# Softmax sums by a chain of adds, one ones product per batch, and a normalization that takes two head groups at a time

## The chip, the cores and the metric

The kernel runs on one core of one Trainium2 chip. TensorE (PE in the profile) does the matrix products, VectorE (DVE), ScalarE (ACT) and GpSimd (POOL) the elementwise work, and SyncE (SP) issues most transfers. The metric is the device time of one execution in microseconds; lower is better. The time before is given as the median of three runs.

## What is computed

Two sequences of 1024 rows of 1024 numbers pass through half a feed-forward layer (a base product plus a gated low-rank part), a causal attention with 32 query heads and 8 key/value heads, and the same half feed-forward layer again. Each of the three parts adds to the residual stream and starts with a layer norm. The change lies in the attention alone:

```python
qg = q.reshape(B, N_KV_HEADS, GROUP, T, D_HEAD)
att = jnp.einsum('bhgqd,bhkd->bhgqk', qg.astype(jnp.float32), k.astype(jnp.float32)) / math.sqrt(D_HEAD)
causal = jnp.tril(jnp.ones((T, T), dtype=bool))
att = jnp.where(causal[None, None, None], att, -jnp.inf)
probs = jax.nn.softmax(att, axis=-1).astype(resid.dtype)
ctx = jnp.einsum('bhgqk,bhkd->bhgqd', probs, v)
```

`GROUP` is 4, `D_HEAD` 32, T 1024.

## The kernel before

The 2048 rows are 16 tiles of 128 rows (t = 0 to 15), eight per sequence. The attention goes through them in the order 0 to 7, 9 to 15, 8; one such stretch of time is called the step of tile t here. A tile sees L = t mod 8 + 1 key tiles, so L runs from 1 to 8. Inside a step, the eight key/value heads are called groups, g = 0 to 7; a group holds four query heads. A (tile, group, key tile) triple is a unit; there are 576 of them.

For each unit, TensorE makes the scores twice: a first time (`unit_s1`, L645) for the row maxima, which VectorE reduces out of PSUM (L662), and a second time (`unit_s2`, L796) with the maxima folded into the operands, from which ScalarE takes the exponentials `p32` (L802), a tile of 128 keys by four heads of 128 queries in float32. On the diagonal key tile GpSimd clears what the causal mask forbids (L804). Between the units, pieces of dense work for neighbouring tiles are dealt out (`step`): feed-forward products, the q/k/v products, the output projection (L404 to L406), three half-precision products for each block of 128.

The weights `p32` are gathered by `av_add` into batches of up to `BATCH = 4` key tiles of one group: batches of 4 and 4 for L = 8, of 4 and 3 for L = 7, of 4 and 1 for L = 5, one batch for L up to 4. When a later batch has begun, `add_pairs` adds the batch's weights two by two on VectorE (L718, tile `pair`, two buffers); an odd one is left as it is. When the later batches hold `SKEW = 2` units, `av_batch` issues the batch's products on TensorE (L739): for each key tile four products with the value tile, one for each head in its own 32 columns of the array, into `av[:, 0, :]`, and then for each pair (or odd left-over) four products with a block of ones, into `av[:, 1, :]`, which so collects the softmax denominators, equal in all 32 rows of a head. A float32 product shows as two instructions in the profile, so one such set of four heads is eight of them. The products of a batch are tied in order (`issue_after`) and have high priority.

After the last batch of a group comes its normalization (L745 to L757): ScalarE copies both halves of `av` to SBUF (L746), VectorE takes the reciprocal of the 128x128 sums (L748) and multiplies (L753), ScalarE rounds the result to half precision (L754, `c.high(g)`), and GpSimd subtracts to get the low part (L755, `c.low(g)`). The two halves of eight groups are the operand of the output projection (`stage_c1`). The PSUM pool `p_av` has one buffer, which takes a whole bank whatever the tile's size; the next group's first product has to wait until the copy L746 has read it. The pool is also used by the first feed-forward passes (`ffn` with `first`).

The framework builds the order of instructions on each engine at compile time: it simulates a timeline with its own costs and takes, for each engine, what is ready in that timeline, by priority. Within an engine the chip then runs that fixed order and waits wherever an operand is late. Where two engines touch one PSUM tile, the framework puts a wait between them.

Of the kernel before, what the change touches and what calls it, by code (L numbers as in the profile page):

```python
# [9 lines left out]
FP = mybir.dt.float32  # L10
# [3 lines left out]
ALU = mybir.AluOpType  # L14
# [3 lines left out]
NH, NKV, DH, GRP = 32, 8, 32, 4  # L18
E, R = 8, 16
P = 128  # L20
KB = D // P
# [20 lines left out]
def kernel(  # L42
# [16 lines left out]
    nc = tc.nc  # L59
# [5 lines left out]
    small = ctx.enter_context(tc.tile_pool(name="small", bufs=SB))  # L65
# [11 lines left out]
    p_av = ctx.enter_context(tc.tile_pool(name="p_av", bufs=1, space=bass.MemoryType.PSUM))  # L77
# [321 lines left out]
    def dense(ps, tt, wsel, n=512, last=True):  # L399

        for k in range(KB):
            wh, wl = wsel(k)
            th, tl = tt.high(k), tt.low(k)
            nc.tensor.matmul(ps, lhsT=th, rhs=wh, start=(k == 0), stop=False)  # L404
            nc.tensor.matmul(ps, lhsT=th, rhs=wl, start=False, stop=False)  # L405
            nc.tensor.matmul(ps, lhsT=tl, rhs=wh, start=False, stop=(last and k == KB - 1))  # L406
            if k % 2 == 1:
                yield
# [26 lines left out]

    def ffn(xt, tt, done, first=False):
        if first:
            psa = p_av.tile([P, 2, P], FP, name="av").rearrange("p a q -> p (a q)")
        else:
            psa = p_dense.tile([P, 512], FP, name="pd")  # L440
        yield from dense(psa[:, 0 : P + E], tt, lambda k: (ag[:, 0, k, :], ag[:, 1, k, :]))
        nc.gpsimd.dma_start(out=xt, in_=hb.partition_broadcast(P), accum_op=ALU.add)

        lg = small.tile([P, E], FP, name="lg")
        nc.scalar.activation(lg, psa[:, P : P + E], AF.Copy, scale=S["cg"])
        nv = small.tile([P, 1], FP, name="nv")
        nc.vector.tensor_reduce(nv, lg, AX.X, ALU.max, negate=True)
        ex = small.tile([P, E], FP, name="ex")
        nc.scalar.activation(ex, lg, AF.Exp, bias=nv)
        fe = lg.unsqueeze(1).to_broadcast([P, E, E])  # L450
        ee = lg.unsqueeze(2).to_broadcast([P, E, E])
        lw = small.tile([P, E, R], FP, name="lw", bufs=1)
        gt, eq = lw[:, :, 0:E], lw[:, :, E : 2 * E]
        nc.vector.tensor_tensor(gt, fe, ee, ALU.is_gt)
        nc.vector.tensor_tensor(eq, fe, ee, ALU.is_equal)
        nc.vector.tensor_tensor(eq, eq, tri, ALU.mult)
        nc.vector.tensor_tensor(gt, gt, eq, ALU.add)
        rk = small.tile([P, E], FP, name="rk")
        nc.vector.tensor_reduce(rk, gt, AX.X, ALU.add)
        nc.vector.scalar_tensor_tensor(ex, rk, 1.5, ex, ALU.is_lt, ALU.mult)  # L460
        sm = small.tile([P, 1], FP, name="sm")
        nc.vector.tensor_reduce(sm, ex, AX.X, ALU.add)
        nc.vector.reciprocal(sm, sm)
        nc.vector.tensor_scalar(ex, ex, sm, S["inva2"], ALU.mult, ALU.mult)
        nc.vector.tensor_tensor(
            lw, psa[:, 0:P].rearrange("p (e r) -> p e r", r=R),
            ex.unsqueeze(2).to_broadcast([P, E, R]), ALU.mult,
        )
        yield True
        psb = [None, None]  # L470
        lh = ll = None
        for n in range(2):
            ps = p_dense.tile([P, 512], FP, name="pd")
            psb[n] = ps
            yield from dense(
                ps, tt, lambda k: (wb[:, n, 0, k, :], wb[:, n, 1, k, :]), last=False
            )
            if n == 0:
                pst = p_s1.tile([P, GRP, P], FP, name="s1")[:, 0, :]
                nc.tensor.transpose(pst, lw.rearrange("p e r -> p (e r)"), ident)  # L480
                lh = small.tile([P, P], HP, name="lh", bufs=LB)
                ll = small.tile([P, P], HP, name="ll", bufs=LB)
                nc.scalar.copy(lh, pst)
                nc.vector.tensor_tensor(ll, pst, lh, ALU.subtract)
                yield
            c = bass.ts(n, 512)
            nc.tensor.matmul(ps, lhsT=lh, rhs=lbh[:, c], start=False, stop=False)  # L487
            nc.tensor.matmul(ps, lhsT=lh, rhs=lbl[:, c], start=False, stop=False)
            nc.tensor.matmul(ps, lhsT=ll, rhs=lbh[:, c], start=False, stop=True)
            yield  # L490
            nc.vector.scalar_tensor_tensor(xt[:, c], ps, S["uf", n], xt[:, c], ALU.mult, ALU.add)  # L491
            done(n)
            if n == 0:
                yield True

    def stage_a1(t):
        tt = layernorm(xts[t], turn=t < NTURN)
        yield

        def done(n):  # L500
            if n == 1:
                Ts["x2", t] = layernorm(xts[t])
                if t == LATE:
                    late["x"] = dram.tile([P, D], FP, name="xlate")
                    nc.sync.dma_start(out=late["x"], in_=xts.pop(t))

        yield from ffn(xts[t], tt, done, first=t < NTURN)
        yield True
# [24 lines left out]
    KT, VA, QS, CTX, CT = {}, {}, {}, {}, {}  # L533
# [168 lines left out]
    avt = [None]  # L702

    pairs = {}

    def add_pairs(batch):

        t, g, L, us = batch
        key = (t, g, us[0][0])
        if key in pairs:  # L710
            return
        pairs[key] = []
        for i in range(0, len(us), 2):
            if i + 1 == len(us):
                pairs[key].append(us[i][1])
                continue
            sums = pp.tile([P, GRP, P], FP, name="pair", bufs=2)
            nc.vector.tensor_tensor(sums, us[i][1], us[i + 1][1], ALU.add)  # L718
            pairs[key].append(sums)

    def av_batch():

        add_pairs(pend[0])
        t, g, L, us = pend.popleft()
        if us[0][0] == 0:
            avt[0] = p_av.tile([P, 2, P], FP, name="av")
        av = avt[0]
        last = us[-1][0] == L - 1
        runs = [(0, VA[t - t % TPB + j][:, g, :], p32) for j, p32 in reversed(us)]
        runs += [(1, ones, sums) for sums in reversed(pairs.pop((t, g, us[0][0])))]  # L730
        prev = None
        for n, (i, w, p32) in enumerate(runs):
            for h in range(GRP):
                rows = slice(h * DH, (h + 1) * DH)
                with ExitStack() as st:
                    if prev is not None:
                        st.enter_context(tc.high_priority())
                        st.enter_context(tc.issue_after(prev.ins))
                    prev = nc.tensor.matmul(  # L739
                        av[rows, i, :], lhsT=w, rhs=p32[:, h, :],  # L740
                        start=(us[0][0] == 0 and n == 0), stop=(last and n == len(runs) - 1),
                        skip_group_check=True, tile_position=(0, h * DH),
                    )
        if last:
            o = pp.tile([P, 2, P], FP, name="o", bufs=2)  # L745
            nc.scalar.copy(o, av)  # L746
            rc = o[:, 1, :]
            nc.vector.reciprocal(rc, rc)  # L748
            if t not in CTX:
                CTX[t] = Halves()  # L750
            c = CTX[t]
            o2 = pp.tile([P, P], FP, name="o2", bufs=1)
            nc.vector.tensor_tensor(o2, o[:, 0, :], rc, ALU.mult)  # L753
            nc.scalar.copy(c.high(g), o2)  # L754
            nc.gpsimd.tensor_tensor(c.low(g), o2, c.high(g), ALU.subtract)  # L755
            if g == NKV - 1:
                CT[t] = CTX.pop(t)  # L757

    def av_add(t, g, j, L, p32):

# [65 lines left out]
    def stage_c2(t):  # L826
        xt = xts[t]

        def done(n):
            if t == LATE:  # L830
                c = bass.ts(n, 512)
                nc.sync.dma_start(out=of[bass.ts(t, P), c], in_=xt[:, c])
            elif n == 1:
                nc.sync.dma_start(out=of[bass.ts(t, P), :], in_=xt)

        yield from ffn(xt, Ts.pop(("x3", t)), done)
        xts.pop(t)
        for u in {LATE - 1: (t + 5, t + 6), NT - 5: (LATE,), LATE: ()}.get(t, (t + 5,)):
            if u < NT:
                load_x(u)  # L840
        yield True
# [89 lines left out]
    pp = ctx.enter_context(tc.tile_pool(name="pp", bufs=2, reuse_waits="tile"))  # L931
# [5 lines left out]
    def flush(_):  # L937
        while pend:
            av_batch()
        yield True  # L940
# [198 lines left out]
```

## Time and profile before

| what | value |
|---|---|
| median of three runs (lowest, highest) | 1507.35 us (1506.07, 1509.0) |
| profiled execution, first to last instruction | 1508.5 us |
| mean granted TensorE clock | 0.978 of full speed |
| second-score products L796 | 576 of 128x512, 385 ns each |
| exponentials L802 | 576 of 128x512, 688 ns each |
| maxima L662, PSUM source | 480 of 128x512, 675 ns each |
| normalization on ScalarE and GpSimd: L746, L754, L755 | 128 each; 372, 297 and 521 ns |

The profiled execution is one execution under the hardware profiler; its span lies 1.2 us above the median of the three runs. Each group of instructions is given by its line, and `out<-in` names the tiles. The duration of a TensorE product contains its way through the array; products follow one another faster than that (in the timeline, dense products of 128x512 start 0.22 us apart and are listed with 0.38 us each), so costs on TensorE are better taken from starts than from durations. The idle time behind the bar in a group's line is what the engine stood still before those instructions, with what ended it.

### The profile page before, as it was taken

Reading aid. Unit: us, or ns where it says so; the run is one execution under the profiler, and the core shown is the slowest. Engines: PE = TensorE matmul, PEld = TensorE weight load, DVE = VectorE, ACT = ScalarE, POOL = GpSimd, SP = SyncE. Lnnn points to the kernel's source line nnn. Section 1 sums busy time; section 2 is a strip of 40 time slices with the busy share of each in tenths; the row PEclk is TensorE's granted clock in tenths of the full one; section 3 lists DMA queues with packets and bytes.
Section 4 is the critical chain, followed back from the end, with each engine's and each line's share of the span. In section 5 each row is a group of like instructions: output and inputs, shape, how many; then the busy total and the mean of one; then the engine's idle time right before and its main releaser. Section 6 shows DMA issues by size and latency. Waiting matters only on the chain.

```text
span 1508.5 us, 35338 instructions
## 1 busy us (share of the span) xinstructions
PE 1407.3 (93%) x14596; PEld 787.6 (52%) x14596; DVE 1136.9 (75%) x2411; ACT 749.4 (50%) x1356; POOL 388.6 (26%) x642
## 2 busy tenths in 40 slices
PE   5877889989999999999999898999999999989998
PEld 3333445545555555565654454555555556556544
DVE  6876957777869789688863687886869689789753
ACT  8563435444545455465561334553645456556531
POOL 3442224222322222222120133322322122221120
PEclk9998999999999999999999899999999999999999
DMA  8989187468487874846658858669595863923552
GB/s 294 324 193 245 24 214 192 141 166 261 90 285 87 237 186 85 258 114 141 192 145 269 181 185 239 188 162 264 105 297 78 242 162 87 275 82 86 127 163 76
DMA packets 265266, 269.40 MB, mean 179 GB/s; under 512 B 227472, under 2 KB 230544, under 8 KB 245392
## 3 DMA queue, kind: packets, MB, share of 16 engines
q1 hardware_dynamic: 259024, 239.87, 57.3%
q0 software_dynamic: 4640, 16.78, 6.5%
q10 hardware_dynamic: 1440, 10.49, 1.9%
q8 instruction: 114, 1.87, 0.5%
q14 instruction: 48, 0.39, 0.1%
HBM read 191.60 MB, written 20.45 MB: 141 GB/s over the span
## 4 chain that ended last, share of the span: by engine, by line
PE 68%; DVE 13%; DMA 10%; ACT 3%; issue 3%; POOL 1%; SPq 1%; ACTq 0%; DVEq 0%; POOLq 0%
PE pd L404 13%; PE pd L405 13%; PE pd L406 13%; PE av L739 11%; PE s L796 6%; PE s L645 6%; DMA ws<-wstr 4%; DVE mx L662 4%; DMA tt<-hl 3%; DVE pair L718 2%; DMA qt<-qst 1%; DVE o L748 1%; ACT p L802 1%; DVE bst L374 1%; PE pd L487 1%
## 5 line engine op out<-in xcount | busy, mean ns | idle before, releaser
L802 ACT ACTIVATE p<-s,cs 128x512 f32<-128x512 f32 x576 | 380.8, 688 | 266.9 <-PE s L796 260.4
L662 DVE TENSOR_REDUCE mx<-s 128x4 f32<-128x512 f32 x480 | 315.5, 675 | 55.7 <-PE s L645 45.4
L718 DVE TENSOR_TENSOR pair<-p,p 128x512 f32<-128x512 f32 x256 | 178.0, 697 | 62.3 <-ACT p L802 30.9
L645 PE MATMUL s<-kts,qt 96*128 96x128 f16 x2304 | 217.9, 221 | 7.1 <-DVE mx L662 2.6
L796 PE MATMUL s<-qt,kts 128*128 128x512 f16 x576 | 211.0, 385 | 11.8 <-ACT p L802 5.8
L404 PE MATMUL pd<-ws,tt 128*128 128x512 f16 x544 | 208.8, 384 | 14.1 <-DMA ws<-wstr 11.5
L645 PEld LDWEIGHTS <-qt 96*128 96x128 f16 x2304 | 165.4, 99 | 100.7 <-issue 30.1
L405 PE MATMUL pd<-ws,tt 128*128 128x512 f16 x544 | 208.2, 383 | 0.0
L406 PE MATMUL pd<-ws,tt 128*128 128x512 f16 x544 | 207.3, 382 | 0.0
L404 PE MATMUL pd<-wb,tt 128*128 128x512 f16 x512 | 197.9, 387 | 8.5 <-DVE xt L491 5.0
L404 PEld LDWEIGHTS <-tt 128*128 128x128 f16 x1312 | 130.5, 99 | 139.3 <-DMA tt<-hl 14.9
L405 PE MATMUL pd<-wb,tt 128*128 128x512 f16 x512 | 197.1, 385 | 1.4 <-DVE wb L213 1.4
L405 PEld LDWEIGHTS <-tt 128*128 128x128 f16 x1312 | 130.8, 100 | 128.7 <-issue 24.2
L406 PE MATMUL pd<-wb,tt 128*128 128x512 f16 x512 | 197.1, 385 | 0.0
L406 PEld LDWEIGHTS <-tt 128*128 128x128 f16 x1312 | 130.5, 100 | 125.0 <-issue 10.6
L739 PE MATMUL av<-p,va 128*32 128x128 f32 x4608 | 166.9, 278 | 4.6 <-ACT o L746 2.6
L804 POOL TENSOR_SCALAR_AFFINE_SELECT p<-p 128x512 f32<-128x512 f32 x128 | 90.7, 712 | 234.9 <-ACT p L802 228.3
L739 PEld LDWEIGHTS av<-p,va 128*32 128x32 f32 x4608 | 115.6, 110 | 68.1 <-issue 52.9
L755 POOL TENSOR_TENSOR tt<-o,tt 128x128 f16<-128x128 f32 x128 | 66.6, 521 | 325.9 <-ACT tt L754 325.8
L748 DVE RECIPROCAL o<-o 128x128 f32<-128x128 f32 x128 | 120.8, 944 | 21.4 <-ACT o L746 21.2
L657 POOL TENSOR_SCALAR_AFFINE_SELECT sm<-sm 128x512 f32<-128x512 f32 x96 | 66.2, 689 | 203.1 <-ACT sm L656 198.0
L754 ACT CAST tt<-o 128x128 f16<-128x128 f32 x128 | 38.0, 297 | 110.0 <-DVE o L753 105.8
(203 smaller groups left out, 1891.1 us busy)
## 6 DMA issues: line engine op xcount, KB each, us to landing
ws<-wstr SPq DMA_DIRECT2D x142, 1024.0 KB, 5.8
xt<-hb POOLq DMA_DIRECT2D x32, 512.0 KB, 6.3
wstr<-ws ACTq DMA_DIRECT2D x9, 1024.0 KB, 6.1
xt<-in_x_dram SPq DMA_DIRECT2D x16, 512.0 KB, 3.9
out_dram<-xt SPq DMA_DIRECT2D x15, 512.0 KB, 2.9
ws<-in_wb_dram SPq DMA_DIRECT2D x2, 1024.0 KB, 8.7
qst<-in_wb_dram SPq DMA_DIRECT2D x2, 1024.0 KB, 13.2
st<-in_wo_dram SPq DMA_DIRECT2D x2, 1024.0 KB, 14.4
```

Source lines behind the costliest of these rows:

```text
L404: nc.tensor.matmul(ps, lhsT=th, rhs=wh, start=(k == 0), stop=False)
L405: nc.tensor.matmul(ps, lhsT=th, rhs=wl, start=False, stop=False)
L406: nc.tensor.matmul(ps, lhsT=tl, rhs=wh, start=False, stop=(last and k == KB - 1))
L645: nc.tensor.matmul(ps[:, h, :], lhsT=q[0 : 3 * DH, h, :], rhs=KT[b0 + j][0 : 3 * DH, g, :], start=(not pem or h == 0), stop=not pem,)
L662: nc.vector.tensor_reduce(mx[:, odd, j, :], ps, AX.X, ALU.max)
L718: nc.vector.tensor_tensor(sums, us[i][1], us[i + 1][1], ALU.add)
L739: prev = nc.tensor.matmul(av[rows, i, :], lhsT=w, rhs=p32[:, h, :], start=(us[0][0] == 0 and n == 0), stop=(last and n == len(runs) - 1), ...
L748: nc.vector.reciprocal(rc, rc)
L755: nc.gpsimd.tensor_tensor(c.low(g), o2, c.high(g), ALU.subtract)
L796: ins = nc.tensor.matmul(ps.rearrange("p h k -> p (h k)"), lhsT=KT[b0 + j][:, g, :], rhs=q.rearrange("p h k -> p (h k)"), start=True, stop ...
L802: nc.scalar.activation(p32, ps, AF.Exp, scale=cs)
L804: nc.gpsimd.affine_select(out=p32, in_=p32, compare_op=ALU.is_ge, fill=0.0, base=0, pattern=[[0, GRP], [1, P]], channel_multiplier=-1,)
```

## The change

`add_pairs` adds all weights of a batch, up to four, one after another into one tile `pair`, which now has three buffers; a batch of one is left as it is. So `av_batch` has one ones product (eight instructions) for each batch. The PSUM tile `av` holds two neighbouring groups, even and odd, 128x512 in all, and the normalization runs once for the two, after the odd one's last batch. It copies the two value halves on ScalarE, transposes the two sum halves in blocks of 32x32 on VectorE straight from PSUM, takes the reciprocal of one column for each block (eight numbers in a row of the tile), spreads each back over 32 columns in a second transpose, multiplies, rounds and subtracts. Its working tile is one buffer of `pair`; the tiles `o` and `o2` are gone.

```diff
@@ ffn
-            psa = p_av.tile([P, 2, P], FP, name="av").rearrange("p a q -> p (a q)")
+            psa = p_av.tile([P, 2, 2, P], FP, name="av").rearrange("p g a q -> p (g a q)")
@@ add_pairs
-        pairs[key] = []
-        for i in range(0, len(us), 2):
-            if i + 1 == len(us):
-                pairs[key].append(us[i][1])
-                continue
-            sums = pp.tile([P, GRP, P], FP, name="pair", bufs=2)
-            nc.vector.tensor_tensor(sums, us[i][1], us[i + 1][1], ALU.add)
-            pairs[key].append(sums)
+        if len(us) == 1:
+            pairs[key] = [us[0][1]]
+            return
+        sums = pp.tile([P, GRP, P], FP, name="pair", bufs=3)
+        nc.vector.tensor_tensor(sums, us[0][1], us[1][1], ALU.add)
+        for _, p32 in us[2:]:
+            nc.vector.tensor_tensor(sums, sums, p32, ALU.add)
+        pairs[key] = [sums]
@@ av_batch
-        if us[0][0] == 0:
-            avt[0] = p_av.tile([P, 2, P], FP, name="av")
-        av = avt[0]
+        odd = g % 2
+        if us[0][0] == 0 and not odd:
+            avt[0] = p_av.tile([P, 2, 2, P], FP, name="av")
+        av = avt[0][:, odd]
...
-        if last:
-            o = pp.tile([P, 2, P], FP, name="o", bufs=2)
-            nc.scalar.copy(o, av)
-            rc = o[:, 1, :]
-            nc.vector.reciprocal(rc, rc)
-            if t not in CTX:
-                CTX[t] = Halves()
-            c = CTX[t]
-            o2 = pp.tile([P, P], FP, name="o2", bufs=1)
-            nc.vector.tensor_tensor(o2, o[:, 0, :], rc, ALU.mult)
-            nc.scalar.copy(c.high(g), o2)
-            nc.gpsimd.tensor_tensor(c.low(g), o2, c.high(g), ALU.subtract)
-            if g == NKV - 1:
-                CT[t] = CTX.pop(t)
+        if last and odd:
+            normalize(t, g - 1, avt[0])
+
+    def normalize(t, g, av):
+
+        w = pp.tile([P, GRP, P], FP, name="pair", bufs=3)
+        o, rc = w[:, 0:2, :], w[:, 2:4, :]
+        nc.scalar.copy(o, av[:, :, 0, :])
+        nc.vector.transpose(rc, av[:, :, 1, :])
+        r = small.tile([P, 2 * P // DH], FP, name="rcol")
+        nc.vector.reciprocal(r, rc.rearrange("p a (b q) -> p (a b) q", q=DH)[:, :, 0])
+        nc.vector.transpose(rc, r.unsqueeze(2).to_broadcast([P, 2 * P // DH, DH]))
+        if t not in CTX:
+            CTX[t] = Halves()
+        c = CTX[t]
+        nc.vector.tensor_tensor(o, o, rc, ALU.mult)
+        hi, lo = c.tt[:, g : g + 2, :], c.tt[:, KB + g : KB + g + 2, :]
+        nc.scalar.copy(hi, o)
+        nc.gpsimd.tensor_tensor(lo, o, hi, ALU.subtract)
+        if g == NKV - 2:
+            CT[t] = CTX.pop(t)
```

## The prediction

> **What bounds the kernel now.** I read the page's busy shares and the chain of waits first, then the engines' busy time step by step, then the groups that the change touches, and last the waits.
>
> ```profile
> PE 1407.3 (93%) x14596; PEld 787.6 (52%) x14596; DVE 1136.9 (75%) x2411; ACT 749.4 (50%) x1356; POOL 388.6 (26%) x642
> PE 68%; DVE 13%; DMA 10%; ACT 3%; issue 3%; POOL 1%; SPq 1%; ACTq 0%; DVEq 0%; POOLq 0%
> PE pd L404 13%; PE pd L405 13%; PE pd L406 13%; PE av L739 11%; PE s L796 6%; PE s L645 6%; DMA ws<-wstr 4%; DVE mx L662 4%; DMA tt<-hl 3%; DVE pair L718 2%; DMA qt<-qst 1%; DVE o L748 1%; ACT p L802 1%; DVE bst L374 1%; PE pd L487 1%
> ```
>
> TensorE sets the end (68% of the chain), and the products that the change thins out, L739, are 11% of it. VectorE, to which work is added, is next. By steps (columns: stretch, length, then busy time of PE, weight loads, DVE, ACT, POOL):
>
> ```profile
> 142.50:171.80 29.30, 22.93 (x246) 12.76 (x246) 26.90 (x57) 10.45 (x27) 9.10 (x18) 0.88 0.23 64
> 1065.60:1157.30 91.70, 90.42 (x1027) 51.71 (x1024) 72.36 (x152) 47.32 (x87) 25.71 (x40) 1.00 0.75 183
> 1252.80:1346.00 93.20, 88.78 (x1129) 52.48 (x1129) 76.29 (x145) 53.16 (x95) 21.38 (x32) 0.96 0.61 169
> 1346.00:1432.90 86.90, 83.03 (x1189) 51.60 (x1187) 74.52 (x145) 51.39 (x92) 15.38 (x24) 0.98 0.37 99
> ```
>
> These are the steps of tiles 0, 12, 14 and 15 (L = 1, 5, 7, 8). In the middle TensorE idles 1.3 of 91.7 us. At the end VectorE comes close: 82% for tile 14 and 86% for tile 15, with 16.9 and 12.4 us free. Tile 0's step belongs to VectorE (92%).
>
> **What a ones product costs TensorE.** In the ordered chain of waits, stretches of L739 come in three sizes (start, length, what):
>
> ```profile
> 1349.85 1.23 PE av L739 x40
> ...
> 1373.17 1.45 PE av L739 x48
> ...
> 1377.79 1.01 PE av L739 x32
> ```
>
> Each further set of eight instructions, one ones product, adds 0.22 us, and a fixed 0.13 us remains. Before, batches of 1, 2, 3 and 4 key tiles have 1, 1, 2 and 2 ones products: summed over L = 1 to 8 that is 20 in each of 16 group sequences (8 groups, 2 sequences), 320 in all. After, there is one for each of the 192 batches. Removed: 128 x 0.22 = 28.2 us of TensorE, none for L up to 2, one in each group for L = 3 to 6, two for L = 7 and 8 (1.8 and 3.5 us a step). The number of batches, and so of entries into the narrow-column products, stays.
>
> Not all of that is on the path. All L739 work is 576 + 320 = 896 sets x 0.22 = 197 us; the chain carries 11% of 1508.5 = 166 us, 84%. I take 84%: **-23.7 us**, with 28.2 as the other bound.
>
> **What VectorE gets.** The rows used:
>
> ```profile
> L718 DVE TENSOR_TENSOR pair<-p,p 128x512 f32<-128x512 f32 x256 | 178.0, 697 | 62.3 <-ACT p L802 30.9 <-PE av L739 20.6 <-POOL p L804 8.8
> L748 DVE RECIPROCAL o<-o 128x128 f32<-128x128 f32 x128 | 120.8, 944 | 21.4 <-ACT o L746 21.2
> L753 DVE TENSOR_TENSOR o<-o 128x128 f32<-128x128 f32 x128 | 40.6, 317 | 2.2 <-POOL tt L755 0.8 <-DVE o L748 0.5
> L517 DVE SCALAR_TENSOR_TENSOR t<-pd,cosT 128x512 f32<-128x512 f32 x32 | 21.9, 686 | 24.7 <-ACT qs L513 24.2
> L517 DVE SCALAR_TENSOR_TENSOR t<-pd,cosT 128x256 f32<-128x256 f32 x16 | 6.7, 420 | 9.1 <-ACT qs L513 8.6
> L463 DVE RECIPROCAL sm<-sm 128x1 f32<-128x1 f32 x32 | 5.0, 156 | 0.6
> ```
>
> Adds: 256 become (0+1+2+3+3+4+5+6) x 16 = 384; 128 x 0.697 = **+89.2 us**. The added ones depend on the add before; in the timeline two independent adds run in 1.28 us together (0.60 from start to start), while dependent small operations (L383, L385, L387) start only 0.03 to 0.05 us after the one before has ended, so 0.60 to 0.74 are the bounds, and I keep 0.697.
>
> The Trainium skill, "VectorE: DVE Perf Modes", section "The DRAIN you can't avoid", says that every operation pays a pipeline flush before the next can start and so that operations should be few. It speaks against this change, which has 640 operations in place of 512. By it all 128 adds cost a full 0.697 (+89.2); by the overlapping pair in this trace they could cost 0.60 (+76.8).
>
> Normalization, per two groups: a transpose of 128x256 out of PSUM, a reciprocal of 128x8, a transpose of 128x256, a multiplication of 128x256. The trace has no VectorE transpose. Its bounds: 0.420 us, as L517 reads 128x256 out of PSUM, and twice L748, 1.89 us, the dearest row per element. I take 0.42, since a transpose moves elements and iterates nothing. The narrow reciprocal lies between L463 (0.156) and L748 (0.944); by the slope between them, 0.156 + 7 x 0.0062 = 0.20. The multiplication is L753 plus 128 elements at L517's slope (0.686 - 0.420)/256 = 1.04 ns: 0.45. Together 1.49 x 64 = 95.4 us against 161.4 for L748 and L753: **-66.0**. VectorE's net is +23.2 us (77% busy); with the dear transpose, 128 x 1.47 = 188 more.
>
> The skill's same page, "The three transpose paths", gives 311 ns for 128x128 of a 16-bit type on VectorE, 444 ns for 256 elements if L517's slope is added (an estimate); by it VectorE's net would be +26. No row here shows it, and it leaves a 32-bit type open.
>
> By step, a group saves 0.52 in the normalization and pays 0.70 for each extra add: eight groups make -4.1 for L = 1, 2; +1.4 for L = 3 to 6; +7.0 for L = 7, 8. In tiles 14 and 15, then, VectorE's free time falls from 16.9 and 12.4 to 9.9 and 5.4 us, so more maxima and adds come late: I take +2 us, bounds 0 and 10. In L = 1, 2, where tile 0 is VectorE's, I take -2, bounds -4 and 0.
>
> ScalarE loses 85.6 - 64 x (0.372 + 0.406, the row of a 128x256 cast, L544) = 36 us, GpSimd 66.6 - 64 x 0.83 (L522, 128x256) = 13.5. Both have spare time (50%, 26%): nothing on the path. No transfer is added, removed or moved.
>
> **The waits that the change makes.**
>
> ```profile
> PE av L739 <- ACT o L746: 2.6, 5, 0.9
> PE av L739 <- DVE pair L718: 1.7, 5, 0.6
> DVE pair L718 <- PE av L739: 20.6, 21, 2.6
> DVE t L517 <- ACT qs L513: 32.8, 20, 4.5
> ```
>
> First, the last add. The single ones product needs it, and everything behind it on TensorE queues (second scores, dense products; ScalarE's exponentials wait for these). From the timeline I took, batch by batch, the end of the last add and the start of the first product that reads a sum: the median slack is 1.1 to 1.9 us for most batch sizes with L of 5 or more, but a quarter have under 0.8. Moving each ready time of the 128 longer batches by 0.75 us (0.69 plus 0.06 for the signal; in odd batches from the diagonal weights, which the chain now includes) and leaving TensorE's order alone, 22 batches would wait 18.3 us in all, 13.2 of it at L = 7, where the diagonal tile is masked just before its products. The compile-time order can put other products there, at the fixed 0.13 us of another entry. Bounds 0 and 18.3; I take **+5**.
>
> Second, the bank. L739 of the next even group waits for two readers: the copy, then the first transpose. The last wait line shows that two engines reading one PSUM tile take turns: L517 uses nothing that L513 made, yet waits for it. So the transpose starts where L748 started, after L746 and in VectorE's queue. With 0.42 added to those starts, the next batch would have begun too early in 11 of 64 places, 10.6 us in all; half of today's 2.6 us of waits for L746 go. Bounds -1.3 and 10.6; I take **+3**.
>
> The third `pair` buffer removes a part of the 20.6 us in which VectorE waits for products: off the path here, bounds -3 and 0, taken as 0. The reciprocal's wait for L746 (21.2 us) becomes the transpose's.
>
> **Sum.** -23.7 + 5 + 3 + 2 - 2 = -15.7; 1508.5 - 15.7 = 1492.8 on the profiled execution, which lies 1.2 above the median: 1491.6, given as **1492 us**.
>
> **Rivals.**
> (a) The whole 28.2 counts, the order hides the new waits, and the eased normalization gives the 4 us and the buffers 3: about 1474. For it: TensorE is full in the middle; against: the thin slack.
> (b) The gain is hidden anyway: TensorE's freed 0.22 us gaps are spent waiting for maxima, scores or weights that come no sooner. The chain's 13% VectorE and 10% transfers speak for it, the full TensorE of tiles 3 to 13 against. A quarter of 23.7 stays: 1508.5 - 6, 1502, and down to nothing.
> (c) Slower: the ones product waits for its last add. 128 products of 0.22 us are removed and 128 batches have a longer chain, so it decides from a mean wait of 0.22 us. One add (0.70) late in half of them is 45 - 28 = +17: 1524. Against it are today's 1.7 us of such waits; for it, that a third add stands behind maxima in a queue that is 80% full.
> (d) Slower: the transpose is dear. At 1.89 us VectorE gains 12 us a step and tiles 5 to 15 are at 90% and over; half of 188 on the path would give some 1575, a third of it 1540.
>
> **How the numbers follow.** Forecast (1483 to 1499) 0.44; (a) 0.16; (b) 0.14, of it 0.06 faster; (c) 0.17; (d) 0.09. About 0.2%, 3 us, is what a measurement can tell from no change: faster 0.66, same 0.08, slower 0.26. The range, 1472 to 1516, goes from all gains of (a) to the forecast with both waits at their bounds, 1523, cut by the rarer half; about 0.17 is left out, mostly (d) and the worse half of (c).
>
> **What would show it.** L739 with 6144 instructions (7168 - 1024) and some 28 us less TensorE work; VectorE near 1160 busy; the first transpose about 0.42. The waits of L739 for the sums should stay near 5 us and those for the normalization near 3. The prediction is wrong if transposes take 0.8 us or more, if the waits for the last add reach 28 us, or if the steps of tiles 3 to 6 don't shorten by 1 to 2 us each.

## The result: half a per cent slower

The changed kernel takes 1517.73 us (median of 8 runs, 1513.91 to 1521.58) against 1507.57 us of the kernel before beside it; the recorded ratio is 1.0052 with a 95% interval of 1.0030 to 1.0074 (the two medians lie 10 us, 0.7%, apart). The prediction was 1492, faster; the measured median lies just outside its range. The profiled execution spans 1514.7 us, 6.2 more than the profile of before.

The profile page after, the three lines that answer to those of before (busy time by engine; the chain of waits by engine and by line):

```profile
PE 1390.4 (92%) x13572; PEld 763.8 (50%) x13572; DVE 1159.9 (77%) x2539; ACT 719.3 (47%) x1228; POOL 383.4 (25%) x578
...
PE 58%; DVE 18%; DMA 10%; issue 5%; ACT 4%; POOL 2%; SPq 1%; ACTq 0%; POOLq 0%; DVEq 0%
PE pd L404 12%; PE pd L405 12%; PE pd L406 11%; PE av L740 8%; DVE mx L662 6%; PE s L804 5%; PE s L645 5%; DMA ws<-wstr 4%; DMA qt<-qst 3%; DMA tt<-hl 3%; DVE pair L718 2%; DVE pair L716 2%; ACT p L810 1%; DVE bst L374 1%; DVE xt L491 1%
```

TensorE's share of the chain fell from 68 to 58%, and VectorE's rose from 13 to 18%. The products of the change (now L740) fell from 11 to 8%. Every part did what the diff says and cost what was reckoned (groups by line: shapes, count, busy us and mean ns, idle before):

```profile
L718 DVE TENSOR_TENSOR pair<-pair,p 128x512 f32<-128x512 f32 x224 | 159.4, 712 | 6.9 <-POOL p L812 3.6 <-ACT p L810 2.2
L716 DVE TENSOR_TENSOR pair<-p,p 128x512 f32<-128x512 f32 x160 | 112.3, 703 | 31.0 <-ACT p L810 22.7 <-POOL p L812 8.1
L753 DVE STREAM_TRANSPOSE pair<-av 128x256 f32<-128x256 f32 x64 | 28.3, 442 | 14.7 <-ACT pair L752 14.6
L756 DVE STREAM_TRANSPOSE pair<-rcol 128x256 f32<-128x256 f32 x64 | 28.0, 438 | 0.4
L760 DVE TENSOR_TENSOR pair<-pair 128x256 f32<-128x256 f32 x64 | 27.7, 433 | 0.5
L755 DVE RECIPROCAL rcol<-pair 128x8 f32<-128x8 f32 x64 | 12.4, 194 | 0.2
```

The transposes take 0.44 us, the narrow reciprocal 0.19, and VectorE's total is 1159.9 us, where 1160 was reckoned. TensorE has 1024 instructions less. What changed besides is how long TensorE waits (the waits of PE: who, for whom, us in total, times, longest):

```profile
PE pd L404 <- DMA ws<-wstr: 14.1, 8, 4.2
PE s L645 <- DVE mx L662: 11.4, 17, 2.9
PE pd L404 <- DMA tt<-hl: 10.2, 5, 3.5
PE s L804 <- ACT p L810: 9.9, 27, 1.1
PE s L804 <- DMA qt<-qst: 9.5, 9, 2.3
...
PE av L740 <- DVE pair L718: 6.8, 14, 1.4
```

and before:

```profile
PE s L796 <- ACT p L802: 5.8, 16, 1.2
PE s L796 <- DMA qt<-qst: 4.8, 5, 1.7
...
PE s L645 <- DVE mx L662: 2.6, 8, 0.8
```

The waits for the maxima were 2.6 us before, those for the exponentials 5.8, for the turned q 4.8, for the sums 1.7. TensorE's idle time as a whole (span less busy time) rose from 101.2 to 124.3 us. And the clock fell (span and mean granted TensorE clock, first before, then after):

```profile
core 0: 1508.5 us, clock 0.978
```

```profile
core 0: 1514.7 us, clock 0.970
```

A mean clock of 0.978 means that (1 - 0.978) x 1508.5 = 33.2 us of TensorE's clock were withheld; after, 0.030 x 1514.7 = 45.4. As an estimate, three terms make up the account: 28.2 us of products gone (128 x 0.22), 23.1 us of idle time and 12.2 us of clock come in, +7.1 in all against the +6.2 of the two spans. The idle time is read from the pages; the clock term is an upper figure, since TensorE stood still for a part of the time at the lower clock.

The steps of tiles 6, 12, 14 and 15 after (stretch, length; PE, weight loads, DVE, ACT, POOL busy; clock, DMA):

```profile
582.10:693.10 111.00, 101.19 (x1117) 59.24 (x1117) 93.70 (x191) 56.59 (x95) 25.58 (x34) 0.96 0.60 155
1073.70:1167.60 93.90, 88.97 (x980) 49.82 (x978) 73.31 (x170) 46.65 (x81) 24.04 (x35) 1.00 0.73 176
1262.70:1354.80 92.10, 85.59 (x986) 48.75 (x985) 78.60 (x152) 50.34 (x86) 18.67 (x28) 0.96 0.65 171
1354.80:1438.20 83.40, 78.94 (x1059) 46.60 (x1056) 78.02 (x156) 49.49 (x83) 14.54 (x20) 1.00 0.40 102
```

Tile 6's step before:

```profile
580.60:682.70 102.10, 100.39 (x1248) 59.64 (x1248) 82.61 (x172) 57.66 (x102) 24.03 (x36) 1.00 0.65 170
```

The late steps, where VectorE was expected to run short, are 1.1 and 3.5 us shorter. The steps of tiles 3 to 6 are longer by 1.6, 5.1, 0.6 and 8.9 us, 16.2 together, while tile 2's is 9.2 shorter. In tile 12's step TensorE now idles 4.9 us where it idled 1.3. Tile 6's step grew from 102.1 to 111.0.

How a full VectorE queue can become lost TensorE time is seen just ahead of tile 6's step (timeline of the changed kernel, rows picked out; start, length, engine, line):

```profile
573.83 1.10 DVE L718 TENSOR_TENSOR pair<-pair,p 128x512 f32<-128x512 f32 x1
...
574.86 0.61 DVE L682 TENSOR_SCALAR qst<-m 128x8 f16<-128x8 f32 x1
...
576.35 0.68 DVE L662 TENSOR_REDUCE mx<-s 128x4 f32<-128x512 f32 x1
576.95 0.68 DVE L718 TENSOR_TENSOR pair<-pair,p 128x512 f32<-128x512 f32 x1
577.08 0.38 PE L645 MATMUL s<-kts,qt 96*128 96x128 f16 x4 [1.91 <-DVE mx L662]
...
577.55 0.18 DVE L683 SCALAR_TENSOR_TENSOR qst<-m,qst 128x8 f16<-128x8 f32 x1
...
577.76 3.40 SPq L625 DMA_TRANSPOSE qt<-qst  x2
...
582.11 1.01 PE L804 MATMUL s<-qt,kts 128*128 128x512 f16 x2 [1.90 <-DMA qt<-qst]
```

VectorE stands still nowhere in these 8 us. L682 and L683 are the two small operations that put the maxima into q. A chain add (L718, 1.10 us) stands ahead of the first, and another add and two maxima stand between the two. Only after the second can the transfer that turns q start, and the tile's first second-scores (L804) wait for that. TensorE waits 1.9 us twice. In the same place the kernel before waits 0.4 and 1.2 us. The first wait is VectorE's queue; the second is so only in part. In the kernel before, the two small operations lie further apart (573.24 and 576.89, with a reciprocal between them), but from the start of the transfers to the second scores it takes 3.5 us there (577.10 to 580.62) and 4.4 here.

### The profile page after: what moved, and what is told of

It reads as the page before. It is cut to its first block, busy times and chain, and to the rows that moved or that the text cites. A ratio compares the mean times of both kernels' runs of the same rounds, so it can differ in the third digit from the quotient of the medians.

```text
span 1514.7 us, 33259 instructions
## 1 busy us (share of the span) xinstructions
PE 1390.4 (92%) x13572; PEld 763.8 (50%) x13572; DVE 1159.9 (77%) x2539; ACT 719.3 (47%) x1228; POOL 383.4 (25%) x578
## 4 chain that ended last, share of the span: by engine, by line
PE 58%; DVE 18%; DMA 10%; issue 5%; ACT 4%; POOL 2%; SPq 1%; ACTq 0%; POOLq 0%; DVEq 0%
PE pd L404 12%; PE pd L405 12%; PE pd L406 11%; PE av L740 8%; DVE mx L662 6%; PE s L804 5%; PE s L645 5%; DMA ws<-wstr 4%; DMA qt<-qst 3%; DMA tt<-hl 3%; DVE pair L718 2%; DVE pair L716 2%; ACT p L810 1%; DVE bst L374 1%; DVE xt L491 1%
## 5 line engine op out<-in xcount | busy, mean ns | idle before, releaser
L804 PE MATMUL s<-qt,kts 128*128 128x512 f16 x576 | 211.6, 387 | 20.9 <-ACT p L810 9.9
L645 PE MATMUL s<-kts,qt 96*128 96x128 f16 x2304 | 213.4, 222 | 18.1 <-DVE mx L662 11.4
L645 PEld LDWEIGHTS <-qt 96*128 96x128 f16 x2304 | 165.3, 99 | 107.2 <-issue 38.2
L404 PEld LDWEIGHTS <-tt 128*128 128x128 f16 x1312 | 130.4, 99 | 134.0 <-issue 13.2
L740 PE MATMUL av<-p,va 128*32 128x128 f32 x4608 | 168.0, 279 | 3.9 <-POOL p L812 2.2
L718 DVE TENSOR_TENSOR pair<-pair,p 128x512 f32<-128x512 f32 x224 | 159.4, 712 | 6.9 <-POOL p L812 3.6
L740 PEld LDWEIGHTS av<-p,va 128*32 128x32 f32 x4608 | 118.7, 111 | 62.8 <-issue 39.5
L716 DVE TENSOR_TENSOR pair<-p,p 128x512 f32<-128x512 f32 x160 | 112.3, 703 | 31.0 <-ACT p L810 22.7
L657 POOL TENSOR_SCALAR_AFFINE_SELECT sm<-sm 128x512 f32<-128x512 f32 x96 | 73.8, 769 | 214.5 <-ACT sm L656 207.8
L656 ACT COPY sm<-s 128x512 f32<-128x512 f32 x96 | 56.1, 585 | 80.8 <-PE s L645 79.7
L330 DVE TENSOR_TENSOR hl<-xn,hl 128x1024 f16<-128x1024 f32 x45 | 59.9, 1330 | 31.4 <-ACT hl L329 28.8
```

The source lines that it names most:

```text
L645: nc.tensor.matmul(ps[:, h, :], lhsT=q[0 : 3 * DH, h, :], rhs=KT[b0 + j][0 : 3 * DH, g, :], start=(not pem or h == 0), stop=not pem,)
L657: nc.gpsimd.affine_select(out=sm, in_=sm, compare_op=ALU.is_ge, fill=-3.0e38, base=0, pattern=[[0, GRP], [-1, P]], channel_multiplier=1,)
L716: nc.vector.tensor_tensor(sums, us[0][1], us[1][1], ALU.add)
L718: nc.vector.tensor_tensor(sums, sums, p32, ALU.add)
L740: prev = nc.tensor.matmul(av[rows, i, :], lhsT=w, rhs=p32[:, h, :], start=(us[0][0] == 0 and n == 0), stop=(last and n == len(runs) - 1), ...
L804: ins = nc.tensor.matmul(ps.rearrange("p h k -> p (h k)"), lhsT=KT[b0 + j][:, g, :], rhs=q.rearrange("p h k -> p (h k)"), start=True, stop ...
```

## Experiments

LOAD stands for: VectorE's added work itself makes the loss, because its queue runs full at places. LAST ADD: only the ones product's wait for the end of the chain matters. NORM: the two-group normalization and its bank make it. BALANCE came after the first runs: a TensorE microsecond counts only as far as VectorE is not what is late. Ratios are to the kernel before, run beside each on the same chip.

### One half of the change at a time

The chain alone, on the kernel before (`pair` keeps its two buffers here):

```diff
-        pairs[key] = []
-        for i in range(0, len(us), 2):
...
+        sums = pp.tile([P, GRP, P], FP, name="pair", bufs=2)
+        nc.vector.tensor_tensor(sums, us[0][1], us[1][1], ALU.add)
+        for _, p32 in us[2:]:
+            nc.vector.tensor_tensor(sums, sums, p32, ALU.add)
+        pairs[key] = [sums]
```

> The kernel before with the chain of adds and one ones product per batch alone (pair keeps two buffers, one a batch); the normalization per group as it was. TensorE loses 28.2 us of products, VectorE gets 89 us of adds and none of the 66 us back. Theory LOAD (VectorE's queue overflows at places, maxima and the transfers behind them come late, TensorE idles and its clock is halved): slower than the changed kernel, 1522 to 1540. Theory LAST ADD (only the ones product's wait for the end of the chain matters): like the changed kernel, 1513 to 1522. Theory NORM (the two-group normalization and its bank make the loss): faster than before, 1485 to 1500.

Measured: 1555.5 us, ratio 1.0293 (1.0257 to 1.0328).

The normalization alone, on the changed kernel:

```diff
+        # add_pairs as in the kernel before: two by two, bufs=2
-        w = pp.tile([P, GRP, P], FP, name="pair", bufs=3)
+        w = pp.tile([P, GRP, P], FP, name="w", bufs=1)
```

> The changed kernel with the adds two by two and all 320 ones products as before (pair two buffers, the normalization's working tile one of its own); the two-group normalization alone. VectorE loses 66 us, TensorE's products stay. LOAD: faster than before, 1492 to 1504, with fewer us of half clock. LAST ADD: like before within 4 us, 1503 to 1510. NORM: slower than before, 1512 to 1522.

Measured: 1487.65 us, ratio 0.9837 (0.9813 to 0.9862); repeated on another chip 1486.49, 0.9854 (0.9832 to 0.9877).

> The normalization alone again, on the chip of the run before this one: 1484 to 1489, so that the chain in tile 7 is worth 0 to 5 us; if it comes out under 1482 the chain in tile 7 is worth nothing.

The change is two changes of opposite sign: the normalization brings some 22 us, and the chain costs 44 us on the old normalization and 30 on the new. NORM falls, and so does LAST ADD, for which the chain alone should have been like the changed kernel. The profile of the normalization alone (busy line, clock, and the waits of PE for maxima and exponentials):

```profile
PE 1395.6 (94%) x14596; PEld 786.8 (53%) x14596; DVE 1080.0 (73%) x2411; ACT 719.7 (48%) x1228; POOL 366.7 (25%) x578
```

```profile
core 0: 1486.8 us, clock 0.983
```

```profile
PE s L645 <- DVE mx L662: 2.7, 6, 0.7
...
PE s L804 <- ACT p L810: 2.0, 8, 0.5
```

VectorE has 57 us less, and TensorE with the same products as before idles 91.2 us in place of 101.2 and loses 25.3 us of clock in place of 33.2.

### Load against wait

In the changed kernel, the first add of each batch alone; and the same with a reduction of each left-out key tile that nobody reads, so that VectorE is loaded but the product waits for the first add only:

```diff
-        nc.vector.tensor_tensor(sums, us[0][1], us[1][1], ALU.add)
-        for _, p32 in us[2:]:
-            nc.vector.tensor_tensor(sums, sums, p32, ALU.add)
+        nc.vector.scalar_tensor_tensor(sums, us[0][1], 1.0, us[1][1], ALU.add, ALU.add)
+        for _, p32 in us[2:]:                                  # second kernel alone
+            rest = small.tile([P, GRP], FP, name="rest")
+            nc.vector.tensor_reduce(rest, p32, AX.X, ALU.add)
```

> The changed kernel with the first add of each batch alone (weights of the third and fourth key tile of a batch are left out of the sums, and 1 is added so that they are not zero): 160 adds in place of 384, TensorE as in the changed kernel. LOAD and LAST ADD: faster than before, 1470 to 1488, since 156 us of VectorE and the wait are gone and the 28 us of products too. NORM: still 1500 or more.

Measured: 1467.82 us, ratio 0.9721 (0.9694 to 0.9747).

> As the run with the first add alone, but each of the 224 left-out adds is replaced by a reduction of the same weights to four numbers that nobody reads (675 ns by the row of the maxima, against 697): VectorE's load is that of the changed kernel, and the ones product waits for the first add alone. LOAD: near the changed kernel, 1508 to 1522. LAST ADD: near the run with the first add alone, under 1492. Halfway, 1495 to 1505, would mean both.

Measured: 1517.57 us, ratio 1.0053 (1.0023 to 1.0082), the changed kernel's 1.0052. The wait for the sums in its profile:

```profile
PE av L741 <- DVE pair L716: 2.1, 4, 0.7
```

With the wait for the last add gone (2.1 us where the changed kernel has 8.0 in all) and the load nearly kept (VectorE busy 1144 us against 1160), nothing is won. Then the load alone on the kernel before, into a tile that is no longer used:

```diff
+        if len(us) > 2:
+            nc.vector.tensor_reduce(hs[:, 0:GRP], us[-1][1], AX.X, ALU.add)
```

> The kernel before with one more VectorE reduction of 128x512 to four numbers that nobody reads, for each of the 128 batches of three or four key tiles: 128 x 0.675 = 86 us of VectorE work and nothing else. LOAD, with the price that the earlier runs give (chain alone +44 us for 89 us of adds less 28 us of products): slower by 40 to 70 us, 1548 to 1578, by idle TensorE and half clock. If what hurts is that TensorE waits for the sums (LAST ADD): under 1515.

Measured: 1554.05 us, ratio 1.0305 (1.0279 to 1.0332): 46 us for 128 x 0.675 = 86 us of work that nobody waits for (VectorE's busy time, in which overlapping rows count once, rose by 66). LOAD stands. The waits of TensorE for the maxima (L645) agree with it: they are 1.4 us in the profile of the first add alone (VectorE busy 1025 us), 2.7 with the normalization alone (1080), 9.0 with the unread sums (1144), 11.4 in the changed kernel (1160), 12.1 with the load alone (1203) and 13.2 with the chain alone (1213); the kernel before has 2.6 at 1137, and 7.6 at 1133 once products are taken off it, as below.

### What the removed products are worth

The same 128 products taken out, with VectorE at three levels of load. First in the kernel before:

```diff
-            nc.vector.tensor_tensor(sums, us[i][1], us[i + 1][1], ALU.add)
+            nc.vector.scalar_tensor_tensor(sums, us[i][1], 1.0, us[i + 1][1], ALU.add, ALU.add)
...
-        runs += [(1, ones, sums) for sums in reversed(pairs.pop((t, g, us[0][0])))]
+        runs += [(1, ones, pairs.pop((t, g, us[0][0]))[0])]
```

> The kernel before with all 256 adds, but only the first ones product of each batch (the later ones, and so some weights in the sums, are left out; 1 is added to the sums): 128 products less on TensorE, VectorE's load unchanged. If TensorE sets the end as I took it, 23 to 28 us faster: 1480 to 1487. If the freed time is spent waiting for VectorE: 1495 to 1507.

Measured: 1509.49 us, ratio 1.0011 (0.9990 to 1.0032). The 28 us are gone from TensorE and nothing is faster. Its profile:

```profile
core 0: 1505.6 us, clock 0.972
```

The clock was 0.978 before; the idle time (span less busy time) is 120.7 us where it was 101.2. So some 19 us came back as idle time and 9 as clock.

The same on the normalization alone:

> The two-group normalization with all 256 adds, but only the first ones product of each batch (the later ones, and so some weights in the sums, are left out; 1 is added to the sums): against the run with the normalization alone, 28 us of TensorE less and nothing else. BALANCE (a removed TensorE microsecond counts only where VectorE is not the one that is late): with VectorE eased by 66 us it is worth more than in the kernel before, where it was worth nothing: 1466 to 1478. If products are never worth anything: 1485 to 1490.

Measured: 1480.24 us, ratio 0.9812 (0.9792 to 0.9832), 4 to 6 us under the two runs of the normalization alone, with overlapping intervals. And with the first add alone, here by putting the products back:

```diff
-        pairs[key] = [sums]
+        pairs[key] = [sums] * ((len(us) + 1) // 2)
```

> The run with the first add alone, but the batches of three and four key tiles issue their ones product twice (the sums are then counted twice there, beside the weights left out): 160 adds and all 320 ones products. Against the run with the first add alone, 28 us of TensorE more and nothing else. BALANCE (the fewer adds on VectorE, the more a TensorE microsecond counts): 1480 to 1492, 12 to 25 us more than 1468, where the same products were worth nothing in the kernel before and 7 us with VectorE at 1080 us. If TensorE products are not worth more than 7 us anywhere: 1470 to 1476.

Measured: 1480.9 us, ratio 0.9811 (0.9783 to 0.9840), 0.9% above the run with the first add alone: 13.6 us, the intervals apart. So the same 28 us are worth about 0, 5 and 14 us with VectorE busy 1137, 1080 and 1025 us. BALANCE agrees with these three, but even the last is only half. One rival is open: every kernel here has its own order of instructions from compile time, and the second of the lookahead runs below changes the time by 0.8% with the same work. The zero and the 5 us are smaller than that.

In the other direction, no adds and a product for each key tile:

```diff
+        pairs[key] = [p32 for _, p32 in us]
```

> The two-group normalization without any adds: a ones product for each key tile (576 in place of 320, +56 us of TensorE), 256 adds less on VectorE (-178 us). If a TensorE microsecond is worth a whole one and VectorE with 66 us less is out of the way: 1487 + 50, 1530 to 1545. If a VectorE microsecond is still worth a third: 1470 to 1490.

Measured: 1514.4 us, ratio 1.0033 (1.0014 to 1.0052), between the two expectations: 27 us more than the normalization alone for 56 us of TensorE work, with 140 us less on VectorE. TensorE is then the one that is full (95%). What VectorE's relief gives back of the 56 us this run doesn't separate. Of the three ways to form the whole sums on the new normalization (no adds, two by two, the chain) two by two is the fastest.

### Ways around

The second add of each chain on GpSimd:

```diff
+        for i, (_, p32) in enumerate(us[2:]):
+            eng = nc.gpsimd if i == 0 else nc.vector
+            eng.tensor_tensor(sums, sums, p32, ALU.add)
```

> The changed kernel with the second add of each chain (128 of 384) on GpSimd in place of VectorE: VectorE's load is that of the run with the normalization alone, TensorE's that of the changed kernel. LOAD: faster than the normalization alone, 1465 to 1485, if GpSimd's adds take 1.5 us beside its other work. If their length comes back as waits for the ones product, or they slow VectorE by sharing its reads: 1490 to 1515.

Measured: 1510.38 us, ratio 1.0013 (0.9997 to 1.0029). The group of these adds in its profile:

```profile
L719 POOL TENSOR_TENSOR pair<-pair,p 128x512 f32<-128x512 f32 x128 | 166.1, 1298 | 233.5 <-ACT p L811 100.7 <-DVE pair L716 60.5 <-DVE mx L662 26.2
```

They take 1.3 us, as hoped, but VectorE is busy 1122.9 us, not 1080: its own instructions got longer. The 128x512 additions of L530 take 926 ns where they take 763 in the run with the normalization alone, the small L682 441 ns where it takes 210. The Trainium skill, "SBUF — State Buffer", section "Who interferes with whom", says that a VectorE instruction with two SBUF inputs contends with a GpSimd instruction that reads SBUF; the longer L530, which adds two SBUF tensors, agrees with it. That is some 5 of the 43 us; L682 has one tensor input, so this sentence doesn't cover it, and the rest is spread over many small operations.

Further lookahead, on the changed kernel and on the kernel before. It changes the computation: the q of tile 8 is asked for in tile 15's step before it has been loaded back, so that the first two groups of tile 8 use another tile's q; the work is the same.

```diff
-LOOK = [6, 6, 4, 4, 3, 3, 3, 3]
+LOOK = [6, 6, 5, 5, 4, 4, 4, 4]
```

> The changed kernel with the maxima one unit of a group further ahead of the second scores for L of 3 and more (LOOK 5, 5, 4, 4, 4, 4 in place of 4, 4, 3, 3, 3, 3). If what VectorE's load costs is a deadline (maxima, then the transfer that turns them, then second scores, at the end of a step), an earlier start takes a good part back: 1495 to 1508. If it is plain lack of VectorE time: 1512 to 1525.

Measured: 1521.33 us, ratio 1.0085 (1.0067 to 1.0104).

> The kernel before with the same lookahead as in the changed kernel with further lookahead, as its control: a deadline gives 1495 to 1508 here too, lack of time 1505 to 1515; the difference between the two says whether the lookahead makes up for the change alone.

Measured: 1519.54 us, ratio 1.0077 (1.0060 to 1.0094). Earlier maxima help neither: the control loses 0.8%, the changed kernel 0.3% more than without them. Between the two only 2 us are left of the change, with overlapping intervals, so a part of its loss may well be such a deadline at the ends of the steps. These runs do not say which stretch loses what.

The chain in tile 7's step alone, beside the normalization:

```diff
+        if t == LATE - 1:
+            # the chain and one product, as in the changed kernel
...
```

> The normalization alone, with the chain and one product per batch in tile 7 only, the step in which VectorE is busy 67%: 16 adds more (11 us), 16 products less (3.5 us). BALANCE: 1483 to 1488, up to 3.5 us faster than the normalization alone. LOAD without regard to the place: 1489 to 1493.

Measured: 1482.2 us, ratio 0.9827 (0.9809 to 0.9846).

> The normalization alone with the chain in tile 7 only, again, beside the next run on one chip: 1480 to 1486.

Measured: 1485.94 us, 0.9849 (0.9828 to 0.9871), beside the normalization alone with 0.9854. The two can't be told apart. Either is 1.5% faster than the kernel before, and the normalization alone is the simpler.

## Why the prediction was wrong

**The price of the removed products** is the step that failed: "I take 84%: -23.7 us", from the share of L739 in the chain of waits. Measured alone on the kernel before, it is 0 (ratio 1.0011, 0.9990 to 1.0032); with VectorE eased it is 5 and 14 us. The chain tells where one execution's time went, not what is saved when a piece of it is made shorter: TensorE and VectorE feed each other unit by unit (scores, maxima, turned q, second scores, exponentials, products), and what one saves it can lose in waiting for the other. Rival (b) said this, at 0.14, but with no loss in it. Rivals (c) and (d) had the direction, by causes that the runs exclude: no rival had what happened.

**VectorE's net** was reckoned rightly in size (+23.2, measured 1159.9 - 1136.9 = 23.0) and wrongly in price. I put it at +2 in tiles 14 and 15 and -2 in L = 1 and 2. For tiles 6 and 7, which get the same +7.0 by the prediction's own table, and for L = 3 to 6 the sum has no term. The runs give 0.2 to 0.5 us of time for each us on VectorE: 14 for 96 adds or 67 us at the lowest load (0.9721 to 0.9812, with TensorE's products thinned), 36 for the next 128 adds or 89 us (0.9812 to the changed kernel's 1.0052), 46 for 86 in the kernel before. The total load does not settle the price: with the same thinned products, the old normalization instead of the new (VectorE 1079 to 1133) costs 30 us, and from there to the changed kernel (1160) it is only 0.4%, some 6 us. And the loss fell in the steps of tiles 3 to 6, not in the late ones. The prediction had named it as a sign of being wrong if these didn't shorten by 1 to 2 us each.

**The wait for the last add** (+5, rival (c)): the waits are there, 8.0 us for L718 and L716 together against 1.7, but they decide nothing. Taken out with the load nearly kept, the time is unchanged (1.0053). **The bank** (+3): 1.7 us of waits for L753, and the normalization that brings them is the faster half.

**Rival (d)**, the dear transpose, is excluded by 442 and 438 ns. (Its "tiles 5 to 15 at 90% and over" also passed over tile 7, whose VectorE was busy 67%.) The estimate by the row of L517 (420) was right, and the one from the Trainium skill's "VectorE: DVE Perf Modes", section "The three transpose paths" (444), closer still.

**Left out altogether** was the clock. The profiled execution is 34 us longer than 1508.5 less the removed products; up to 12 of these are clock, which no term of the sum contained.

Put as a ladder from one run to the next (so the sum is no test of it): the normalization about -23 (-1.5 and -1.6% in two runs), then the removed products -5, then the 128 adds +36, which is the measured +8. In this order the miss of some 24 us (-15.7 forecast, +8 measured) is 19 from the price of the products and 13 from VectorE's net, less the 8 put down for two waits that cost nothing.

## What to carry to other kernels

When one engine is full and the next is four fifths full and they feed each other, price each by an experiment: leave out a piece of the work, or add some that nobody reads. A share of the chain of waits is not the price of the work in it (24 us were expected here; 0, 5 and 14 came), and free time on the second engine is no cover where its queue runs full in bursts. And when a change has two halves, run each alone: here the half that looked like the supporting one was worth 1.5%, and the one it made room for took it back.

## What the runs showed of the hardware

In every profile here TensorE's granted clock is either full or half, and all its changes fall on a grid of 3.41 us. Short waits are enough to halve it. The stretches of the grid at tile 6's step in the changed kernel (stretch, length; PE, weight loads, DVE, ACT, POOL; clock, DMA; the windows lie within 0.1 us of the grid, hence 0.51 and 0.99):

```profile
575.00:578.40 3.40, 1.27 (x32) 0.85 (x28) 3.40 (x11) 0.00 (x0) 0.43 (x1) 1.00 0.00 0
578.40:581.80 3.40, 1.80 (x24) 1.07 (x17) 3.40 (x12) 0.96 (x2) 0.63 (x1) 0.51 1.00 118
581.80:585.20 3.40, 3.10 (x8) 1.13 (x8) 1.73 (x7) 2.44 (x4) 0.00 (x0) 0.50 0.21 41
585.20:588.60 3.40, 3.40 (x26) 1.85 (x24) 1.50 (x4) 2.06 (x4) 0.00 (x0) 0.99 0.00 0
```

and the same place before:

```profile
578.20:581.60 3.40, 1.96 (x17) 1.26 (x17) 3.40 (x9) 1.45 (x3) 1.11 (x2) 1.00 0.94 144
581.60:585.00 3.40, 3.40 (x24) 1.38 (x22) 2.83 (x10) 1.48 (x4) 0.00 (x0) 1.00 0.05 10
```

Busy 1.27 of 3.40 us (37%) at full clock, and the next stretch runs at half; busy 1.80 (53%) at half, and the next stays there; busy 1.96 (58%) at full clock, and the next is full too. Over the 17 profiles of this study, of the stretches of the grid at full clock with TensorE busy under 40%, 192 of 194 are followed by one at half clock (the other two are at 39.5% and 39.9%), of those between 40 and 55% about half (81 of 153), of those at 65% and more none of 6541. So a wait of 2 us can cost up to 1.7 us more, half of 3.41, when it tips a stretch. In all three pairs of runs the profile without the 128 products has the lower clock: 0.972 against 0.978, 0.975 against 0.983, 0.981 against 0.987. Products that fill TensorE without being needed had thus paid for a part of their time.
